# The second layer's last twelve ticks: three steps of norms, gates and experts in a tick instead of two

## The chip, the cores and the metric

The kernel runs on one core of one Trainium2 chip. The metric is the device time of one execution in microseconds (us); lower is better. Five engines work side by side, each through its own instructions in order: PE (TensorE, matmuls; its weight loads are listed apart as PEld), DVE (VectorE), ACT (ScalarE), POOL (GpSimd) and SP (SyncE, which here only starts transfers). The order of an engine's instructions is fixed when the program is built.

## The reference

Two layers, each a graph network followed by a mixture of experts, all with a residual, over 6250 nodes of 256 values. The change is in the second layer:

```python
# L1_gnn
h = relu(x @ Wp.T + bp)
hp = h ** 2
msgs = edge_vals[:, None] * hp[src]
agg = segment_sum(msgs, dst, num_segments=N) ** 0.5
x = x + (h @ W1.T + b1 + agg @ W2.T + b2)
# L1_ffn, on the layer norm of x
all_out = experts_mlp(x)             # 4 experts, 256 -> 128 -> 64 -> 256, relu between
shared = shared_mlp(x)               # 256 -> 256 -> 128 -> 256
gates = softmax(x @ gW + gb)
topv, topi = top_k(gates, 2)
x = x + shared + sum(softmax(topv) * all_out[topi])
```

There are 106250 edges, sorted by destination.

## The kernel before

The 6250 nodes lie in 49 node tiles of 128; the edges, 128 to a tile, make 831 edge tiles. The second layer works on blocks of node tiles (L2155): ten blocks of four, then three of two (40-41, 42-43, 44-45) and three of one (46, 47, 48). The edges come in groups of six tiles, 139 groups. One loop, a tick for each group, carries everything:

- `fetch` issues on POOL an indirect DMA for each edge tile (L1104): the rows `hp[src]` land in `hg`. It runs four groups ahead.
- `weights_of` builds on DVE for each edge tile a matrix `eq` of 128 edges by 96 nodes, the edge's weight where its destination is (L2390). It runs one group ahead.
- `add_up` multiplies on PE `hg` by `eq` into the PSUM tile `pe` of the block that the nodes belong to (L2411); an edge tile whose 96 nodes reach over a block's end needs two matmuls. A block is zeroed by a matmul at its start (L2406). When its last edge tile is in, it is complete.
- `roots` takes on ACT the square root of a complete block (L2428, `gt`).
- `end_of2`, one generator for each node tile, has four steps: the matmuls with W1 and W2 (`w1t`, `w2t` into a `pt`), the add into `x_all` (L2229), mean and variance (L2231, L2233), `ln_rs` (L2235) and a square root on ACT (L2236); reciprocal, `off` and the normalized tile `xn` (L2238, L2240, L2242); its transposes on PE and the copy into `b_all` on ACT (L1085, L1086); the logits on PE and DVE (L1091, L2248).
- `gates2`, one for each block, has five steps of small DVE operations, with an exponential on ACT after the first (L2259) and the fourth (L2295), up to `gate` (L2302).
- `experts2`, one for each block: eleven steps up to the last hidden layer (the shared layers `h1`, `h2` and for each expert `first` and `then`, each a matmul into a `ph` and a relu: L2318, L2326, L2331, L2340), then, once the gates are there, three steps for each node tile that multiply into `py` and add into `x_all` on DVE (L2364, L2366), and last the store to the output (L2373).

`mm` (L1091) issues all matmuls but the add-up's, so most of them have that one line. The `ph` and `py` tiles have two buffers each, `pt` has one.

Generators wait in lists: `ends` (all of them advance by one in a `step_ends`, which also starts one node tile's `end_of2` if one is due), `routes` (gates) and `layers` (experts); `advance(queue, n)` takes n steps of the first in a list. After the loop come the flag checks (L2482 to L2500). From `LATE` = 104 on, a tick has two `step_ends`, two steps of gates and four of experts; before that one, one and three. The builder then places each engine's instructions in its own order, in which neighbouring steps are interleaved. After tick 138 no group is left and the loop runs on until all lists are empty.

Square root and exponential need different function tables on ACT; a change between them shows in the profile as an `ACT_TABLE_LOAD`.

Of the kernel before, what the change touches and what calls it, by code (L numbers as in the profile page):

```python
# [841 lines left out]
def kernel(ctx: ExitStack, tc: tile.TileContext, a: dict, out: bass.AP):  # L842
# [74 lines left out]
    with ExitStack() as fast:  # L917
# [48 lines left out]
        if T1 > C1:  # L966
            V.memset(flat.bitcast(I32)[:, C1:T1], 2**24)
            n = E1 - C1 * P
# [311 lines left out]
        with ExitStack() as layer:  # L1280
# [81 lines left out]
            with (  # L1362
# [61 lines left out]
                def add_up(q):  # L1424

                    w, g = groups1[q]
                    if g == 0:
                        sums[w] = pse.tile([P, WS], F32, name="pe")
                    h, eq = hbuf[q % 2], equals.pop(q)

                    for j in reversed(range(NT)):
                        for i, k in ((1, g + NG), (0, g)):
                            lo, hi = quarters(w, k)
                            if hi - lo == 4:
                                TE.matmul(
                                    sums[w], eq[k][:, j, :], h[:, i * NT + j, :],
                                    start=g == 0 and j == NT - 1 and i == 1,
                                    stop=g == NG - 1 and j == 0 and i == 0,
                                )
                                continue  # L1440
                            for b in range(lo, hi):
                                at = slice((b - lo) * Q, (b - lo + 1) * Q)
                                TE.matmul(  # L1443
                                    sums[w][b * Q : (b + 1) * Q, :], eq[k][:, j, at],
                                    h[:, i * NT + j, :], start=g == 0 and j == NT - 1,
                                    stop=g == last_of[b] and j == 0,
                                )
# [202 lines left out]
        def advance(queue, n):  # L1650
            for _ in range(n):
                if queue and next(queue[0], queue) is queue:
                    queue.pop(0)

        layers = [experts1()]
        part = sums.tile([P, 3, T, H], BF16, name="part")
        with (
# [33 lines left out]
            def fetch(g):  # L1691
                got[g] = wk.tile([P, G, GW], F32, name="sg", bufs=5)
                for j in range(G):
                    gather(got[g][:, j, :], gat_dram, src2[:, g * G + j : g * G + j + 1])
# [447 lines left out]
            k = NA + 5  # L2142
# [14 lines left out]
        with (  # L2157
# [62 lines left out]
            def end_of2(b, i, root):  # L2220


                w = blocks[b][0] + i
                pm = psm.tile([P, D], F32, name="pt")
                mm(
                    pm, lambda c: (b_all[:, w, 0:P], root[:, i, :])[c],
                    lambda c: (w1t, w2t)[c],
                )
                V.tensor_add(x_all[:, w, :], x_all[:, w, :], pm)  # L2229
                st = wk.tile([P, 6], F32, name="ln_st")  # L2230
                V.bn_stats(st, x_all[:, w, :])  # L2231
                mv = wk.tile([P, 2], F32, name="ln_mv")
                V.bn_aggr(mv, st)  # L2233
                rs = wk.tile([P, 1], F32, name="ln_rs")
                V.tensor_scalar(rs, mv[:, 1:2], EPS, None, op0=OP.add)  # L2235
                SC.activation(rs, rs, AF.Sqrt)  # L2236
                yield
                V.reciprocal(rs, rs)  # L2238
                off = wk.tile([P, 1], F32, name="off")
                V.tensor_scalar(off, mv[:, 0:1], rs, -1.0, op0=OP.mult, op1=OP.mult)  # L2240
                xn = wk.tile([P, D], F32, name="xn")
                SC.activation(xn, x_all[:, w, :], AF.Identity, bias=off, scale=rs)  # L2242
                yield
                transposed(psm, b_all[:, w, :], xn)
                yield
                pg = psm.tile([P, D], F32, name="pt")
                mm(pg[:, 0:NX], lambda c: b_all[:, w, c * P : (c + 1) * P], lambda c: gw[:, c, :])
                V.tensor_add(logits(b)[:, i * NX : (i + 1) * NX], pg[:, 0:NX], gb)  # L2248
# [126 lines left out]
            groups2 = [range(t, min(t + G1, T1)) for t in range(0, T1, G1)]  # L2375
# [10 lines left out]
            def weights_of(k):  # L2386

                equals[k] = wk.tile([P, G1, NW], F32, name="eq", bufs=3)
                for j, t in enumerate(groups2[k]):
                    V.tensor_scalar(  # L2390
                        equals[k][:, j, :], lanes[:, 0:NW], dst_of[:, t : t + 1],
                        ew[:, t : t + 1], op0=OP.is_equal, op1=OP.mult,
                    )
# [25 lines left out]
            def roots(b):  # L2419
                n = blocks[b][1]  # L2420
                at = slice(blocks[b][0], blocks[b][0] + n)
                V.tensor_add(
                    x_all[:, at, :], x_all[:, at, :],
                    b12[:, None, :].to_broadcast([P, n, D]),
                )
                root = wk.tile([P, BT, P], F32, name="gt")[:, 0:n, :]
                pe = sums.pop(b)[:, 0 : n * P].rearrange("p (w k) -> p w k", k=P)
                SC.activation(root, pe, AF.Sqrt)  # L2428
                return [(b, i, root) for i in range(n)]

            complete, ends, coming, routes, layers, routed = [], [], [], [], [], set()
            ended = [0] * len(blocks)

            def step_ends(k):
                for item in list(ends):
                    if next(item[1], ends) is ends:
                        ends.remove(item)
                        b = item[0]
                        ended[b] += 1
                        if ended[b] == blocks[b][1]:  # L2440
                            routes.append(gates2(b))
                            layers.append(experts2(b))
                if coming and (k % 2 or coming[0][0] * BT >= small):
                    b, i, root = coming.pop(0)
                    ends.append((b, end_of2(b, i, root)))

            LATE = len(groups2) * 3 // 4

            AHEAD = 4
            for k in range(AHEAD):
# [2 lines left out]
            k = 0  # L2455
            while k < len(groups2) or complete or coming or ends or routes or layers:
                if k + AHEAD < len(groups2):
                    fetch(k + AHEAD)
                if k + 1 < len(groups2):
                    weights_of(k + 1)  # L2460
                if k < len(groups2):
                    add_up(k)
                advance(layers, 1)
                step_ends(k)
                if k >= LATE:
                    advance(layers, 1)
                    advance(routes, 1)
                while complete:
                    coming += roots(complete.pop(0))
                advance(routes, 1)  # L2470
                advance(layers, 2)
                if k >= LATE:
                    step_ends(k)
                k += 1


        with (
# [6 lines left out]
            n = wk.tile([P, NB + 7], F32, name="n")  # L2484
# [4 lines left out]
            for i in range(2):  # L2489
                k = NB + 1 + 2 * i  # L2490
# [55 lines left out]
```

## Time and profile before

| | us |
|---|---|
| runs | 3552.38, 3555.01, 3555.68 (median 3555.01) |
| profiled execution | 3555.79 |
| its span, first to last instruction | 3554.0 |
| second layer's loop: start of the first gather to the start of the last | 2467.6 to 3505.4 |
| start of the last add into `x_all` | 3544.4 |

Busy times over the whole span:

| engine | busy us | share |
|---|---|---|
| PE | 3338.9 | 94% |
| DVE | 2170.1 | 61% |
| ACT | 1412.1 | 40% |
| POOL | 2252.3 | 63% |

The shares are means over stages with different limits. In the second layer POOL issues one gather after the other, 831 of them; PE works on add-ups, norms, gates and experts in between. The mean granted clock of TensorE over the span is 0.911; in the loop from 2508 us to the end it is 0.73. Times in the text are counted from the start of the span.

### The profile page before, as it was taken

What the parts mean: (1) busy time and instruction counts of PE and PEld (TensorE: products, weight loads), DVE (VectorE), ACT (ScalarE), POOL (GpSimd) and SP (SyncE); (2) the same over time, 40 slices, a digit from 0 to 9 for tenths busy, and PEclk for the clock granted to TensorE, in tenths of its full rate; (3) what the DMA queues carried; (4) which work ended last, traced back from release to release, by engine and by line L of the source; (5) the groups of instructions that cost most, each with busy time, mean ns of one, the idle gap of its engine ahead of it and who ended that gap; (6) DMA issues with size and microseconds to landing.
All of it is one profiled execution on the core that took longest, in us unless ns stands there. A gap on an engine that the chain in (4) does not pass through costs nothing.

```text
span 3554.0 us, 57573 instructions
## 1 busy us (share of the span) xinstructions
PE 3338.9 (94%) x20063; PEld 2662.0 (75%) x20063; DVE 2170.1 (61%) x6210; ACT 1412.1 (40%) x2750; POOL 2252.3 (63%) x2367
## 2 busy tenths in 40 slices
PE   7999999999999999999999999997678988989898
PEld 3577777777777778888888888895456666666677
DVE  9999996444544444787758576977234444444464
ACT  4444444444444444444544454664011212211133
POOL 0376666666666664676656555662777777777773
PEclk9999999999999999999999999998567776777797
DMA  6456656656555554433434343553112222222221
GB/s 174 128 189 189 184 183 184 186 186 182 183 183 188 181 183 142 110 97 96 125 88 127 83 130 84 154 94 109 52 53 59 60 59 59 59 59 60 65 62 37
DMA packets 342928, 428.52 MB, mean 121 GB/s; under 512 B 139174, under 2 KB 246453, under 8 KB 342630
## 3 DMA queue, kind: packets, MB, share of 16 engines
q1 hardware_dynamic: 245174, 244.98, 22.1%
q0 software_dynamic: 89408, 178.08, 19.4%
q8 instruction: 162, 2.65, 0.3%
q10 hardware_dynamic: 8048, 1.68, 0.2%
q14 instruction: 136, 1.11, 0.1%
HBM read 382.05 MB, written 42.49 MB: 119 GB/s over the span
## 4 chain that ended last, share of the span: by engine, by line
PE 66%; POOL 14%; DMA 7%; issue 7%; DVE 4%; ACT 1%; SPq 0%; ACTq 0%; POOLq 0%; DVEq 0%
PE ph L1091 32%; POOL hg L1104 13%; PE py L1091 10%; PE pt L1085 7%; PE pe L1443 6%; PE po L1771 5%; DMA hg<-hp_dram,src 5%; PE pt L1091 2%; DMA rb<-low_dram 1%; PE pe L2411 1%; PE pa L1708 1%; PE pm L1091 1%; DVE junk L982 1%; DVE key L1240 0%; DVE order L1237 0%
## 5 line engine op out<-in xcount | busy, mean ns | idle before, releaser
L1104 POOL DMA_INDIRECT yg<-y_dram,src x882 | 847.0, 960 | 543.1 <-issue 226.7
L1104 POOL DMA_INDIRECT hg<-hp_dram,src x831 | 785.7, 946 | 269.2 <-issue 224.3
L1104 POOL DMA_INDIRECT sg<-gat_dram,src x640 | 614.1, 960 | 350.1 <-issue 161.5
L1091 PE MATMUL ph<-w1b,et 128*128 128x256 f32 x3528 | 835.7, 380 | 0.0
L1091 PEld LDWEIGHTS ph<-w1b,et 128*128 128x128 f32 x3528 | 637.0, 190 | 68.7
L2411 PE MATMUL pe<-eq,hg 128*128 128x96 f32 (+15 forms) x2036 | 439.9, 353 | 148.9 <-DMA hg<-hp_dram,src 120.6
L2411 PEld LDWEIGHTS pe<-eq,hg 128*128 128x128 f32 x2036 | 388.2, 260 | 251.8 <-issue 94.6
L1417 DVE TENSOR_TENSOR yg<-ph,yg 128x512 f32<-128x512 f32 x441 | 303.3, 688 | 375.3 <-PE ph L1091 370.7
L2390 DVE TENSOR_SCALAR eq<-px,dst,ew 128x96 f32<-128x96 f32 x831 | 262.0, 370 | 217.2 <-PE pe L2411 120.6
L1091 PE MATMUL ph<-b_all,w 128*128 128x256 f32 (+1 forms) x1600 | 387.1, 380 | 1.5 <-ACT hh L1607 1.4
L1091 PE MATMUL py<-w,hh 128*128 128x256 f32 x1568 | 383.1, 384 | 5.0 <-ACT hh L1607 4.5
L1086 ACT ACTIVATE et<-pt 128x512 f32<-128x512 f32 x441 | 262.2, 596 | 254.4 <-PE pt L1085 242.1
L1422 ACT ACTIVATE h<-yg 128x512 f32<-128x512 f32 x441 | 276.1, 626 | 215.4 <-DVE yg L1417 209.0
L1091 PEld LDWEIGHTS py<-w,hh 128*128 128x128 f32 x1568 | 288.7, 190 | 41.2 <-ACT hh L1607 6.6
L1091 PEld LDWEIGHTS ph<-b_all,w 128*128 128x128 f32 x1600 | 290.0, 190 | 33.7 <-ACT hh L1607 2.0
L1607 ACT ACTIVATE hh<-ph,b 128x256 f32<-128x256 f32 (+1 forms) x400 | 166.7, 467 | 285.6 <-PE ph L1091 279.7
L1085 PE MATMUL pt<-ident,ea 128*128 128x128 f32 x1764 | 272.1, 277 | 3.4 <-ACT et L1086 3.4
L1085 PEld LDWEIGHTS pt<-ident,ea 128*128 128x128 f32 x1764 | 210.2, 144 | 65.0 <-issue 40.4
L1771 PE MATMUL po<-pp,B 128*128 128x240 f32 (+10 forms) x1280 | 252.1, 337 | 2.2 <-DVE acc L1777 2.1
L1771 PEld LDWEIGHTS po<-pp,B 128*128 128x128 f32 x1280 | 215.6, 190 | 14.3 <-DVE acc L1777 2.8
L1443 PE MATMUL pe<-h,eq 128*32 128x257 f32 x3168 | 216.8, 384 | 3.7 <-ACT h L1422 1.9
L1443 PEld LDWEIGHTS pe<-h,eq 128*32 128x32 f32 x3168 | 96.2, 109 | 102.6 <-issue 35.0
(330 smaller groups left out, 4264.5 us busy)
## 6 DMA issues: line engine op xcount, KB each, us to landing
ea<-in_edge_attr_dram SPq DMA_DIRECT2D x147, 768.0 KB
y<-y SPq DMA_DIRECT2D x196, 128.0 KB
w<-in_L_ffn_W_dram SPq DMA_DIRECT2D x48, 512.0 KB
y<-ys SPq DMA_DIRECT2D x96, 256.0 KB
rb<-low_dram SPq DMA_DIRECT2D x80, 256.0 KB
yg<-y_dram,src POOLq DMA_INDIRECT x882
hg<-hp_dram,src POOLq DMA_INDIRECT x831
sg<-gat_dram,src POOLq DMA_INDIRECT x640
```

The lines of the kernel that those rows point to most:

```text
L982: V.tensor_scalar(junk, flat, float(w * P), None, op0=OP.is_lt, op1=OP.add, accum_out=below[:, w : w + 1],)
L1085: TE.transpose(pt[:, c, :], src[:, c * P : (c + 1) * P], ident)
L1086: SC.activation(dst, pt.rearrange("p c k -> p (c k)"), AF.Copy)
L1091: TE.matmul(dst, lhs(c), rhs(c), start=c == 0, stop=c == n - 1)
L1104: GP.indirect_dma_start(out=dst, out_offset=None, in_=table[0:NP, :], in_offset=IndirectOffsetOnAxis(ap=idx, axis=0),)
L1417: V.tensor_add(y, ph, y)
L1422: SC.activation(h[:, j : j + 2, 0:D], y, AF.Relu)
L1443: TE.matmul(sums[w][b * Q : (b + 1) * Q, :], eq[k][:, j, at], h[:, i * NT + j, :], start=g == 0 and j == NT - 1, stop=g == last_of[b] and ...
L1607: SC.activation(hidden[u][:, f, :n, :], ph[:, f - f0, :n, :], AF.Gelu, bias=b1[:, e, f : f + 1],)
L1771: TE.matmul(po.rearrange("p b v -> p (b v)"), B[:, j, :], pp[:, j, 0:n, :].rearrange("p b v -> p (b v)"), start=half == 0 and j == 0, stop ...
L2390: V.tensor_scalar(equals[k][:, j, :], lanes[:, 0:NW], dst_of[:, t : t + 1], ew[:, t : t + 1], op0=OP.is_equal, op1=OP.mult,)
L2411: TE.matmul(sums[b][:, lo - t0 * P : hi - t0 * P], hg[:, j, :], eq[:, j, lo - n0 : hi - n0], start=False, stop=after >= (t0 + n) * P,)
```

## The change

The body of the tick is written as a loop of one, two (from tick 104) or three (from tick 127, `LAST12`) rounds; a round has one step of the first experts, one `step_ends`, one step of the first gates and one more step of the experts (two in a tick before 104). The roots are taken in the first round. So from tick 127 on, also in the ticks behind the last group, a tick has three `step_ends`, three steps of gates and six of experts, where it had two, two and four. From 104 to 126 the numbers are as before, but the second step of gates comes after the second `step_ends` instead of ahead of it, and the fourth step of the experts too; in all ticks the first step of gates now comes ahead of the roots.

```diff
-            LATE = len(groups2) * 3 // 4
+            LATE, LAST12 = len(groups2) * 3 // 4, len(groups2) - 12
...
-                advance(layers, 1)
-                step_ends(k)
-                if k >= LATE:
+                for n in range(1 + (k >= LATE) + (k >= LAST12)):
                     advance(layers, 1)
+                    step_ends(k)
                     advance(routes, 1)
-                while complete:
-                    coming += roots(complete.pop(0))
-                advance(routes, 1)
-                advance(layers, 2)
-                if k >= LATE:
-                    step_ends(k)
+                    if n == 0:
+                        while complete:
+                            coming += roots(complete.pop(0))
+                    advance(layers, 2 if k < LATE else 1)
                 k += 1
```

No operation is added or removed; the same work is issued in another order.

## The prediction

> **What bounds the kernel now.** I read the chain of waits over the last 250 us first, then POOL's, PE's and DVE's timelines, then busy time and clock window by window. From 3331.9 to 3463.0 the chain is POOL issuing the gathers of L1104, one every 1.25 us, and their landing; from 3465.5 on it is PE.
>
> ```profile
> 3460.45 0.94 POOL hg L1104
> 3461.70 0.94 POOL hg L1104
> 3462.95 2.46 DMA hg<-hp_dram,src
> 3465.54 1.02 PE pe L2411 x4
> ```
>
> Columns: start, length, what. Before 3465 an earlier expert step would be ready sooner and change nothing, since PE waits for gathers anyway.
>
> ```profile
> 3505.38 0.94 POOL L1104 DMA_INDIRECT hg<-hp_dram,src  x1 [0.30 <-issue]
> 3512.81 0.36 PE L2411 MATMUL pe<-eq,hg 128*128 128x96 f32 x2
> ...
> 3544.39 0.48 DVE L2366 SCALAR_TENSOR_TENSOR x_all<-py,gate,x_all 128x256 f32<-128x256 f32 x1
> ```
>
> The last gather starts at 3505.4 and, with the 2.46 us above, lands at 3507.9. The last add-up matmul (pe) ends at 3513.2, so PE is 5 us behind the gathers. The last add into x_all ends at 3544.9; store and flag check take the other 9.1 us of the span of 3554.0, and no line of the change touches them. At stake are the 31.7 us from the last add-up to the last add, and PE's delay before.
>
> ```profile
> 3460.94:3464.35 3.41, 2.03 (x15) 1.73 (x13) 2.88 (x9) 0.00 (x0) 2.50 (x4) 1.00 0.17 49
> 3464.35:3467.76 3.41, 3.11 (x13) 2.85 (x13) 0.00 (x0) 0.00 (x0) 2.67 (x3) 0.50 0.20 58
> 3491.65:3495.06 3.41, 3.41 (x10) 2.69 (x9) 0.76 (x5) 2.30 (x4) 2.80 (x3) 0.50 0.19 58
> 3495.06:3498.47 3.41, 3.41 (x23) 3.18 (x22) 1.92 (x7) 0.88 (x2) 2.50 (x4) 0.99 0.18 52
> 3464.35:3495.06 30.71, 30.39 (x110) 27.14 (x111) 9.55 (x39) 4.80 (x11) 23.39 (x25) 0.50 0.22 62
> ```
>
> Columns: window, length, busy of PE, weight load, DVE, ACT, POOL, then granted clock, DMA share, GB/s. The clock is 1.0 or 0.5 and changes only at steps of 3.41 us. A window with PE busy 2.03 us was followed by half clock; full clock came back after a window filled with 256-column expert matmuls. Cutting everything from 2600 us on into such windows, each full-clock window with 2.2 us or less busy was followed by half clock, and none with more than 3.0. So 30.7 us before the end ran at half clock.
>
> **The change, part by part.** I number blocks by node tiles: 44-45, 46, 47, 48 are the last four.
>
> *Ticks before 127* only change order inside a tick. Cost 0: POOL's chain hides it (POOL waits for nothing but its own issue, 0.30 us each). Without that cover, one expert step of 0.4 to 0.9 us would show.
>
> *Ticks 127 to 130.* Block 42-43 is finished in tick 130 instead of 132. Ticks 131 to 133 then hold little but gathers; PE idles there and is at half clock when it leaves tick 133. The last gather of that tick is 27 before the end: 3505.4 - 27 x 1.25 + 2.5 = 3474.1, so PE, with one pe more, is free at about 3474.5. Before, the same point came at 3476.7.
>
> *From there to the last add-up.* In the built order of PE, blocks 44-45 and 46 stand ahead of the last add-up almost whole; before, five output matmuls of 44-45 and all of 46 stood behind. At full-clock durations (spacings of PE's timeline): 42 pe at 0.23 = 9.7; 28 matmuls of 256 columns at 0.43 = 12.0; four L2329 of two tiles at 0.57 = 2.3; block 46's 14 of 128 columns at 0.22 = 3.1, four at 0.36 = 1.4, four outputs at 0.43 = 1.7; transposes, logits, zeroing 2.4. Sum 32.6. Half clock lasts until a filled window. From about 3479 eight 256-column matmuls stand together, 7.1 us at the half-clock 0.89 (3490.1 to 3493.7 shows four in 3.56), long enough to hold one, so release at 3482 to 3486, I take 3484: 9.5 us at half speed, penalty 4.8. Waits for ACT 0.6 (half a table load of 1.28). New is a wait on DVE: the last tick's three eq (L2390) now stand behind node 47's add, statistics and rs (0.42 + 0.43 + 0.17 + 0.14), which wait for PE's w2t matmul of node 47; the last three pe wait for these eq: 1.2 + 0.3 for the first, 1.5 in all. Last add-up: 3474.5 + 32.6 + 4.8 + 0.6 + 1.5 = 3514.0, 0.8 later than before.
>
> *Behind it.* Before, 25.5 us of PE work, 5.3 of waits, 0.9 from the last matmul to the last add. Off go five outputs of 44-45 (2.1) and block 46 (0.9 + 1.8 + 0.45 + 1.4 + 2.2 = 6.8): 16.6 left. Waits: node 47's xn, behind the three eq (0.94), share (0.48), reciprocal and off (0.37) on DVE and 0.59 on ACT, leaves PE idle 1.6; its copy 0.45; two table loads (1.28 each) ahead of block 47's relus cost 0.9, since the third ph must wait for a relu to free one of two buffers; another ahead of block 48's relus 0.9; handoffs 0.5: 4.4. At the end the share's exp (L2295) of block 48 now stands behind ACT's last relu, before it stood ahead: exp 0.16, five DVE steps 1.0, then the four adds 2.2: 3.5 after the last matmul instead of 0.9. So 16.6 + 4.4 + 3.5 = 24.5 instead of 31.7: -7.2, with the 0.8 above -6.4.
>
> *The clock in the tail.* From w2t of node 47 to its xn are 4.0 us, in which PE has 0.9 us of work. Wherever the 3.41 us windows fall, one holds less than 2.2 us busy, and by the rows above half clock follows. Transposes, logits, h1 and the first two experts of 47 (3.7 us at full clock) then run at half until a filled window two or three later: +2.9 after what the table loads hide. Bounds: 0, and 3.7 plus as much again if the third window isn't filled. I take 2.9: **-3.5**.
>
> [...]
>
> Stores (L2373) of 42 to 47 move ahead with their blocks on SP's queue, which has nothing else there; the last store stays last. No DMA on POOL moves. If stores weren't hidden, only the last one (inside the 9.1 us) would tell.
>
> The profiled execution took 3555.8, 1.8 beyond its span; the median is 3555.0. 3555.8 - 3.5 = 3552.3 in its terms, 3551.5 for the median.
>
> **The rivals.**
> 1. *The clock holds and PE catches up with the gathers.* For it: PE stays at full clock in the row 3525.78 with 2.43 us busy, so the limit isn't sharp; ticks 131 to 133 may hold the clock through, removing the 4.8. Against it: the drought there and the 4.0 us above. Last add-up between 3508.2 (last landing plus one pe) and 3514.0, no tail penalty: -6.4 to -12.2, middle -9: 3546.
>
> ```profile
> 3525.78:3529.19 3.41, 2.43 (x18) 1.97 (x16) 2.20 (x11) 3.16 (x9) 0.00 (x0) 1.00 0.14 43
> ```
>
> 2. *Nothing gained.* PE's work is only put in another order, and PE is full from 3465: what leaves the tail (8.9) comes back as delay of the last add-up, at its bound 8.9 - 2.2 (begun earlier) = 6.7, so -0.5: 3554.5. Against it: the 30.7 us at half clock leave room.
> 3. *Slower: half clock from tick 131 to the end.* If add-ups between the expert steps keep every window from being filled (as from 3464 to 3491, busy all the time and yet half), 11 us more at half speed until 3495 cost 5.5, and a tail of 16.6 all at half about 10: -6.4 + 5.5 + 10 = +9: 3564. It decides once over 13 us of PE work more than I count run at half clock. Against it: eight large matmuls together.
>
> **How the numbers follow.** Forecast 0.41, rival one 0.40, rival two 0.09, rival three 0.10. Forecast's own range 3548 to 3554. The measurement can tell 0.2%, 7.1 us: under 3547.9 is faster, over 3562.1 slower. Rival one gives faster but for its uppermost tenth (0.36 and 0.04), forecast and rival two no change (with that 0.04, 0.54), rival three slower (0.10). The range 3543.5 to 3558 leaves out rival three and an eighth of rival one, 0.15.
>
> **What would show it.** Right: the last gather starts at 3505 as before; last add-up at 3513 to 3515; behind it PE idles some 1.5 us twice, waiting for eq and xn; a half-clock window follows; last add 24 to 29 us after the last add-up. Clock 1.0 throughout the tail is rival one, a last add-up at 3519 or later rival two or three. Wrong altogether if the gathers' spacing grows: then the ticks before 127 weren't free.

## The result, and the profile after

| | before | after |
|---|---|---|
| median of 20 runs, us | 3555.12 (3550.81 to 3560.97) | 3560.34 (3555.28 to 3566.59) |
| ratio of the medians, 95% interval | | 1.0015 (1.0008 to 1.0022) |
| profiled execution, us | 3555.79 | 3566.08 |
| its span | 3554.0 | 3564.3 |
| start of the first gather of the loop | 2467.64 | 2472.49 |
| start of the last gather | 3505.38 | 3512.49 |
| end of the last add-up matmul | 3513.2 | 3527.3 |
| end of the last add into `x_all` | 3544.9 | 3555.4 |

The changed kernel is slower by 2.8 to 7.8 us. The prediction was 3551.5, a gain, with a range up to 3558.0; the measured median is 2.3 us above that. The profiled execution of the changed kernel is within 0.5 us of its slowest run. It enters the loop 4.9 us later, though nothing ahead of the loop was changed, and its gathers take 2.3 us longer. Of that, 2.1 us had come together by gather 780, before a tick with three rounds had begun, and e18 below, which has the same order up to there, took 1037.5 us from the first to the last gather where the kernel before took 1037.7; so this part is scatter between executions. So I compare distances from the start of the last gather, and take 7.1 us (3512.49 - 3505.38) off the times of after to set them beside those of before. From the last gather's start to the end of the span it is 48.6 before and 51.8 after: 3.2 us of the loss lie in the part that the change touches, by this one pair of profiles.

Two windows of each kernel hold nearly all of that. The first reaches from the zeroing of block 44-45's sums (a matmul of L2406, 3375.3 before and 3381.7 after) to the last add-up matmul, the second from there to the last add. Columns as in the prediction: window, length, busy of PE with its matmul records, weight load, DVE, ACT, POOL, then granted clock. Before:

```profile
3375.30:3513.20 137.90, 134.36 (x655) 106.78 (x655) 74.60 (x296) 49.01 (x94) 99.07 (x105) 0.85 0.21 59
3513.20:3544.90 31.70, 29.02 (x168) 22.01 (x167) 21.07 (x105) 20.44 (x51) 0.00 (x0) 1.00 0.05 17
```

After:

```profile
3381.70:3527.30 145.60, 140.64 (x707) 110.39 (x706) 81.04 (x325) 56.10 (x110) 99.72 (x106) 0.88 0.22 58
3527.30:3555.40 28.10, 23.06 (x114) 17.31 (x114) 15.69 (x77) 14.17 (x35) 0.00 (x0) 0.84 0.03 10
```

Some 53 matmul records went from the second window to the first (168 to 114, 655 to 707). What to look at is PE's busy time beside the length: before, PE was busy 134.4 of the first 137.9 us. There was no hole for the work that came.

Cutting both windows where the granted clock changes tells how much of the busy time ran at half clock. In the kernel before four matmuls of 256 columns take 3.56 us at half clock (3490.09 to 3493.65) and two take 0.87 at full (3497.00 to 3497.87), so I call busy time less half of that the *work*, in us at full clock; length = work + idle + half-clock time / 2.

| us | length | work | idle | at half clock |
|---|---|---|---|---|
| before, to the last add-up | 137.9 | 114.1 | 3.5 | 40.5 |
| after, to the last add-up | 145.6 | 123.9 | 5.0 | 33.5 |
| before, behind it | 31.7 | 29.0 | 2.7 | 0 |
| after, behind it | 28.1 | 19.3 | 5.0 | 7.6 |

The work is conserved: 114.1 + 29.0 = 143.1 before, 143.2 after. To the last add-up: 9.8 more work, 1.4 more idle, 3.5 less for half clock (7.0 / 2), 7.7 longer. Behind it: 9.8 less work, 2.4 more idle, 3.8 more for half clock, 3.6 shorter. The first window starts 0.7 earlier against the last gather, and the end behind the last add is 0.2 shorter: 7.7 - 3.6 - 0.7 - 0.2 = 3.2.

Where the clock went in after, by the same windows of 3.41 us:

```profile
3474.70:3478.11 3.41, 3.41 (x14) 2.96 (x12) 2.82 (x11) 0.53 (x2) 2.53 (x3) 0.50 0.42 125
...
3488.35:3491.76 3.41, 3.41 (x10) 2.69 (x9) 0.02 (x1) 0.82 (x2) 2.49 (x4) 0.51 0.20 50
3491.76:3495.18 3.42, 3.42 (x21) 2.86 (x20) 1.51 (x9) 2.33 (x6) 2.51 (x4) 1.00 0.18 46
...
3505.42:3508.83 3.41, 2.80 (x25) 2.66 (x24) 3.35 (x13) 0.75 (x2) 2.49 (x4) 0.99 0.21 55
3508.83:3512.24 3.41, 3.41 (x17) 3.41 (x18) 0.22 (x2) 0.37 (x1) 2.74 (x3) 0.50 0.22 58
3512.24:3515.66 3.42, 3.42 (x13) 2.97 (x13) 1.15 (x3) 0.80 (x3) 0.94 (x1) 0.52 0.24 38
3515.66:3519.07 3.41, 3.41 (x24) 2.94 (x22) 3.09 (x10) 0.95 (x3) 0.00 (x0) 1.00 0.00 0
...
3525.89:3529.31 3.42, 2.48 (x14) 1.89 (x14) 3.14 (x15) 1.21 (x4) 0.00 (x0) 0.99 0.00 0
3529.31:3532.72 3.41, 3.13 (x13) 3.06 (x14) 0.99 (x4) 0.76 (x3) 0.00 (x0) 0.50 0.11 38
```

Three stretches at half clock: the one that began with the drought of ticks 131 to 133 (the ticks that hold little but gathers), a new one from 3508.7 to 3515.6, and the tail's. (One more, at the start of the first window, stands in both kernels, to 3385.9 before and to 3392.7 after, and from 3553.1 on, behind the last wait, the last two matmul records run at half clock.) PE's timeline shows what stands at their beginnings (last column: idle time before the group, and what ended it):

```profile
3506.17 0.65 PE L2411 MATMUL pe<-eq,hg 128*128 128x46 f32 x4 [0.61 <-DVE eq L2390]
...
3526.27 1.03 PE L2411 MATMUL pe<-eq,hg 128*128 128x96 f32 x6 [1.67 <-DVE eq L2390]
3527.66 0.39 PE L2479 MATMUL pg<-good,ones 128*128 128x8 f32 x2 [0.37 <-ACT gt L2428]
...
3529.59 1.01 PE L1091 MATMUL pt<-gw,b_all 128*128 128x4 f32 x4 [0.47 <-ACT b_all L1086]
...
3553.68 1.19 PE L1091 MATMUL py<-ew,g 65*128 65x256 f32 x2 [2.26 <-DVE miss L2488]
```

PE waits for `eq` twice, 0.61 and 1.67 us: DVE builds it in its own order, the second time behind the add and the norm steps of node tile 47 that the third round put ahead of it, the first time behind an add (L2364) and the gate steps. The kernel before has a wait like the first, also behind an add, in a window from 3505.31 on with 2.83 us busy, and kept the full clock:

```profile
3506.91 0.68 PE L2411 MATMUL pe<-eq,hg 128*128 128x1 f32 x4 [0.58 <-DVE eq L2390]
```

So the wait alone does not explain the stretch at 3508.7. The 2.26 at the end is the share of the last block: a `py` buffer comes free only when an add with the gate is done (the releaser named, a flag check's step, stands beside those adds in DVE's order).

### The profile page after: what moved, and what is told of

It reads as the page before. It is cut to its first block, busy times and chain, and to the rows that moved or that the text cites. A ratio compares the mean times of both kernels' runs of the same rounds, so it can differ in the third digit from the quotient of the medians.

```text
span 3564.3 us, 57555 instructions
## 1 busy us (share of the span) xinstructions
PE 3334.0 (94%) x20063; PEld 2653.1 (74%) x20063; DVE 2171.8 (61%) x6210; ACT 1412.8 (40%) x2750; POOL 2257.6 (63%) x2367
## 4 chain that ended last, share of the span: by engine, by line
PE 68%; POOL 12%; issue 7%; DMA 6%; DVE 5%; ACT 2%; SPq 1%; ACTq 0%; DVEq 0%; POOLq 0%
PE ph L1091 32%; POOL hg L1104 12%; PE py L1091 10%; PE pt L1085 7%; PE pe L1443 6%; PE po L1771 5%; DMA hg<-hp_dram,src 3%; PE pt L1091 3%; PE pe L2411 2%; DMA rb<-low_dram 2%; PE pa L1708 1%; PE pm L1091 1%; DVE eq L2390 1%; DVE junk L982 0%; DVE x_all L1952 0%
## 5 line engine op out<-in xcount | busy, mean ns | idle before, releaser
L2411 PEld LDWEIGHTS pe<-eq,hg 128*128 128x128 f32 x2036 | 379.1, 255 | 265.3 <-issue 101.9
```

Source lines behind the costliest of these rows:

```text
L2411: TE.matmul(sums[b][:, lo - t0 * P : hi - t0 * P], hg[:, j, :], eq[:, j, lo - n0 : hi - n0], start=False, stop=after >= (t0 + n) * P,)
```

## The experiments

Theory A: the clock is what the prediction missed; without the new half-clock stretches the change would gain. Theory B: PE is full ahead of the last add-up, so whatever moves there delays it one for one, and the tail, a chain of waits, gives back less. Theory C: it is `eq`, built too late. The expectations use other names: their theory A joins A and B (the third round puts work ahead of the last add-ups, and PE's waits there cost the clock), R1 is the new order inside the ticks, R2 the third round behind the last group, and R3 is theory C. Their distances from the last gather (7 to 9 or 14 to 15.5 us) were meant for a chip like that of the result.

One thing has to be known of the first sixteen runs. They ran on chips on which the kernel before itself takes 4317 to 4361 us. In their profiles PE, DVE and ACT stop at times for several us without a releaser in the trace (PE 8.5 us at once in e12, DVE 8.4 and ACT 14.0 in e13); the chain of waits of the changed kernel there reads

```profile
PE 60%; another core or an unknown queue 13%; DVE 11%; issue 8%; ACT 4%; POOL 2%; DMA 1%; ACTq 0%; SPq 0%; DVEq 0%; POOLq 0%
```

The loop's gathers take 1221 to 1244 us instead of 1038, and PE ends its add-ups 28 to 58 us behind the last gather instead of 8 to 15. Ratios are good to some 0.3% there, twice the effect. What can be read there is what doesn't hang on the pauses: matmul counts, PE's work, and the tail with its clock. The last two runs came on a chip that takes 3555 to 3557.

| run | edit | ratio to before (95%) | last add-up to last add, us |
|---|---|---|---|
| e1 | two rounds | 1.0004 (0.9978 to 1.0030) | 29.95 |
| e3 | third only behind the last group | 1.0017 (0.9996 to 1.0038) | 29.94 |
| e6 | the same | 1.0016 (0.9989 to 1.0043) | 29.95 |
| e2 | third only in ticks 127 to 138 | 1.0045 (1.0024 to 1.0066) | 28.88 |
| e5 | the same | 1.0035 (1.0008 to 1.0062) | 28.11 |
| e13 | the changed kernel | 1.0020 (0.9991 to 1.0049) | 28.10 |
| e4 | `eq` a group earlier | 1.0041 (1.0014 to 1.0068) | 30.95 |
| e7 | the same | 1.0076 (1.0052 to 1.0100) | 30.95 |
| e8 | zero matmuls in the last wait | 1.0048 (1.0022 to 1.0075) | 25.10 |
| e9 | zero matmuls in ticks 132, 133 | 0.9994 (0.9960 to 1.0028) | 28.64 |
| e10 | both, and one in tick 136 | 1.0016 (0.9991 to 1.0041) | 25.44 |
| e14 | the same | 1.0024 (1.0000 to 1.0048) | 25.45 |
| e12 | norms and gates only | 0.9994 (0.9970 to 1.0018) | 24.15 |
| e15 | the same | 1.0015 (0.9990 to 1.0040) | 23.10 |
| e11 | before, zero matmuls in tick 132 | 1.0002 (0.9971 to 1.0033) | 31.71 |
| e16 | the same | 0.9998 (0.9979 to 1.0017) | 31.70 |
| e17 | before (chip at 3557.25) | one run, 3554.96 | 31.70 |
| e18 | gates first (same chip) | one run, 3552.81 | 25.96 |

### The change in halves (e1, e2, e3, e5, e6, e13)

```diff
-                for n in range(1 + (k >= LATE) + (k >= LAST12)):
+                for n in range(1 + (k >= LATE)):                                     # e1
+                for n in range(1 + (k >= LATE) + (LAST12 <= k < len(groups2))):      # e2, e5
+                for n in range(1 + (k >= LATE) + (k >= len(groups2))):               # e3, e6
```

e1: 

> The tick is written as in the changed kernel, but there is never a third round: only the order inside a tick differs from before. Theory A (the third round in ticks 127 to 138 puts expert work ahead of the last add-ups, and PE's waits there cost the clock): as before, ratio 0.999 to 1.0005, last add-up 7 to 9 us after the last gather's start (before 7.8, changed kernel 14.8). Rival R1 (the new order inside the ticks costs it): ratio 1.001 or more, last add-up late as in the changed kernel.

e2: 

> Third round in ticks 127 to 138 alone, two rounds behind the last group. Theory A: as the changed kernel or a little better, ratio 1.001 to 1.002, last add-up 14 to 15.5 us after the last gather's start. Rival R2 (the third round behind the last group costs it, by gates that come late and table loads): ratio 1.000.

e3: 

> Third round behind the last group alone. Theory A: ratio 0.9985 to 1.0005, last add-up 7 to 9 us after the last gather's start, 29 to 32 us from there to the last add. Rival R2: ratio 1.001 or more.

e5: 

> Third round in ticks 127 to 138 alone, again, since the chip of the first four runs stopped all engines at times for reasons the profile doesn't show and took 4361 us for the kernel before. On a chip that takes about 3555 us, theory A (the third round in ticks 127 to 138 puts expert work ahead of the last add-ups and PE's waits there cost the clock): ratio 1.001 to 1.002, last add-up 14 to 15.5 us after the last gather's start (before 7.8). Rival R2 (the third round behind the last group costs it): ratio 1.000.

e6: 

> Third round behind the last group alone, again. Theory A: ratio 0.9985 to 1.0005, last add-up 7 to 9 us after the last gather's start, 29 to 32 us from there to the last add. Rival R2: ratio 1.001 or more. Rival R1 (the new order inside the ticks costs it, which this kernel has too): last add-up 12 us or more after the last gather's start.

e13: 

> The changed kernel once more, on the same chip as the three beside it. If its loss is of the order of work: 1.0010 to 1.0025 of the kernel before. If it is chance in where the clock's windows fall: 0.999 to 1.001.

e3 and e6 are built into the same order of instructions as e1 on all five engines: a third round once the groups are over changes nothing, since there its lists are drained in the same order anyway. So 1.0004, 1.0017 and 1.0016 are one kernel measured three times, and show what a ratio is worth there. The third round in ticks 127 to 138 carries what effect there is: both runs of it lie above 1 with their intervals, and e2 and e5 have the changed kernel's order of instructions, so that they and e13 are one kernel measured three times too (1.0045, 1.0035 and 1.0020). First the windows of e1, then those of e5; the ends of the windows are chosen as above.

```profile
4163.70:4329.80 166.10, 145.37 (x666) 113.34 (x666) 75.73 (x302) 50.88 (x97) 75.94 (x81) 0.80 0.15 39
4329.80:4359.80 30.00, 26.88 (x157) 20.09 (x155) 19.23 (x99) 18.51 (x49) 0.00 (x0) 1.00 0.05 18
```

```profile
4120.90:4297.30 176.40, 152.12 (x707) 116.63 (x706) 81.24 (x325) 56.21 (x110) 76.13 (x81) 0.80 0.14 38
4297.30:4325.40 28.10, 23.04 (x115) 17.17 (x114) 15.67 (x77) 14.20 (x35) 0.00 (x0) 0.83 0.03 10
```

41 records more ahead of the last add-up make that window 10.3 us longer, and taking them from the tail makes it 1.9 shorter. That is theory B's picture, though with pauses in it: the first windows' idle times, 20.7 and 24.3, differ by more than one could call an effect. e13 by itself (1.0020, its interval reaches below 1) can't tell order from chance. Clearer is the stretch from the last gather's start to the last add-up, in which PE idles little (1.6 to 5.6 us): PE's work there is 28.2, 28.2 and 29.7 us in e1, e3 and e6, and 34.6, 35.9 and 35.5 in e5, e13 and e2; the last add-up ends 38.5 to 40.6 us behind that start in the first three, 48.0, 48.0 and 57.5 in the others (e2 has 38 us at half clock there, the others 15 to 19).

### Building `eq` a group earlier (e4, e7)

```diff
-                equals[k] = wk.tile([P, G1, NW], F32, name="eq", bufs=3)
+                equals[k] = wk.tile([P, G1, NW], F32, name="eq", bufs=4)
...
             weights_of(0)
+            weights_of(1)
...
-                if k + 1 < len(groups2):
-                    weights_of(k + 1)
+                if k + 2 < len(groups2):
+                    weights_of(k + 2)
```

e4: 

> The changed kernel with the add-up weights (eq) built two groups ahead and in four buffers, so that on DVE the last group's three no longer stand behind node 47's statistics. Rival R3 (this wait of PE for eq, 1.7 us, and the one of 0.6 us in tick 136 ahead of a half-clock stretch, are the cost): last add-up 9 to 11 us after the last gather's start, ratio 0.999 to 1.000. Theory A in the form that expert work ahead in PE's order costs it whatever the eq do: 13 to 14.5 us, ratio 1.001 or more.

e7: 

> The changed kernel with the add-up weights (eq) built two groups ahead and in four buffers, again. Rival R3 (PE's waits for eq are the cost): last add-up 9 to 11 us after the last gather's start, ratio 0.999 to 1.000. Theory A in the form that expert work ahead in PE's order costs it whatever the eq do: 13 to 14.5 us, ratio 1.001 or more.

Slower than before in both, with intervals wholly above 1. The edit did not take the wait away: ahead of the last add-up PE still waits for `eq`, 3.7 us at once in e4 and 4.4 in e7. And the tail, with the same work as in the changed kernel (19.5), has 8.3 us of idle instead of 5.1, as this answer on PE's waits in e7's tail shows (waiting for whom, total us, times, longest):

```profile
PE py L1091 <- DVE x_all L2366: 2.4, 1, 2.4
PE py L1091 <- DVE miss L2489: 2.3, 1, 2.3
PE ph L1091 <- ACT h L2340: 1.1, 1, 1.1
```

The first of these is not there in e5. From the last gather's start to the last add are 80.8 and 81.4 us, where e5 and e13 have 76.1 (e2, with its 38 us at half clock, 86.4). So this way out of the wait costs more than it saves; theory C itself is not tested by it, since the wait stayed.

### Zero matmuls to hold the clock (e8, e9, e10, e14, and e11, e16 in the kernel before)

They multiply `ident` by zeros: into an unused `pe` buffer behind the last block's root (e8), or into the open sums ahead of add-up matmuls, where they add nothing (the others). Nothing is left out.

```diff
 def roots(b):
+                if b == len(blocks) - 1:                      # e8, e10, e14
+                    warm = pse.tile([P, BT * P], F32, name="pe")
+                    for _ in range(6):
+                        TE.matmul(warm[:, 0:D], ident, nothing[:, 0:D], start=True, stop=True)
...
 def add_up(k):
+                        if k in (132, 133):                   # e9; e10, e14: or k == 136 and j == 0; e11, e16: k == 132
+                            TE.matmul(sums[b][:, 0 : n * P], ident, nothing[:, 0 : n * P],
+                                      start=False, stop=False)
```

e8: 

> The changed kernel with six more matmuls of 256 columns on zeros into a free buffer of the add-up's PSUM pool, results unused; the built order puts five of them into PE's wait for the last three eq and one behind the first of the last add-ups. If the clock in the tail is lost because PE waits there (theory A): clock 1.0 through that wait and behind it, last add 24 to 26 us after the last add-up instead of 28.1, and the time 2 to 3 us under the changed kernel's, ratio 1.0005 to 1.001. If the half clock there costs nothing: 2 us more, ratio 1.0015 to 1.002.

e9: 

> The changed kernel with a 128-column matmul of ident by zeros (adds nothing to the sums) ahead of each add-up matmul of ticks 132 and 133, 19 in all, 4.2 us at full clock, where PE waits for gathers. If the first half-clock stretch (3474.7 to 3491.8 in the profile of after) is what makes the last add-up late, it goes: 8.5 us of half speed saved less at most 3 us of filler that the waits don't hide, so the last add-up ends 6 to 10 us (not 14.8) behind the start of the last gather, and the time is 4 to 6 us under the changed kernel's. If the work of the third round by itself makes it late, the clock holds there but the last add-up stays 13 us or more behind the last gather, and the time stays within 2 us of the changed kernel's. If filler only costs: 2 to 4 us over.

e10: 

> As before, with one more zero matmul ahead of the first add-up matmul of tick 136 (where PE waited 0.61 us for eq ahead of the second half-clock stretch) and six of 256 columns in PE's wait for the last eq. If the clock is what the prediction missed: no half clock from tick 132 to the last add, last add-up 4 to 8 us behind the start of the last gather, last add 24 to 26 us behind that, the time 8 to 12 us under the changed kernel's and 3 to 6 us under the kernel before. If it is the order of the work: only the tail's 3 us are gained, and the time is not under the kernel before.

e14: 

> The changed kernel with 20 zero matmuls of one node tile's 128 columns in ticks 132, 133 and 136 and six of 256 columns in PE's wait for the last eq. If the clock is what the prediction missed: no half clock from tick 134 to the last add, and 6 to 12 us under the changed kernel beside it. If it is the order of the work: 2 to 4 us under it, for the tail alone.

e11: 

> The kernel before with the same zero matmuls ahead of the 10 add-up matmuls of tick 132 (2.2 us at full clock), where its half-clock stretch of 30.7 us began. If the clock alone decides when the last add-up ends: no half clock ahead of 3495, last add-up 3 to 4 us behind the start of the last gather instead of 7.8, and the time 3 to 5 us under the kernel before. If PE, having caught up, waits for gathers and falls to half clock a few windows later: last add-up at 7 us or more, the time within 2 us of the kernel before.

e16: 

> The kernel before with zero matmuls ahead of the 10 add-up matmuls of tick 132. If its half-clock stretch sets the end: 3 to 5 us under the kernel before. If PE then waits for gathers and loses the clock later: within 2 us.

In the tail the clock's price is shown. The second window of e8, beside that of e5 above, has the same count of matmul records:

```profile
4296.70:4321.80 25.10, 19.63 (x115) 14.29 (x114) 15.26 (x73) 13.86 (x35) 0.00 (x0) 1.00 0.03 11
```

1.00 instead of 0.83, and 25.1 us instead of 28.1; in e10 and e14 25.4. So half clock in the tail costs 2.7 to 3.0 us; the prediction had 2.9. The fillers have a price ahead of it: from the start of node tile 47's matmuls with W2 to the end of the last add-up are 3.8 us in e8, 3.3 in the changed kernel of the result. Ahead of the last add-up the fillers did not do what theory A wanted: in e9, e10 and e14 half clock still held for 14 to 20 us that end 33 us ahead of the last gather's start, and for 20 us around that start (52.6 to 60.6 us at half clock in the first window, 52.8 in the changed kernel there). Where fillers stood they did not keep PE busy: in e9 the later of these stretches begins at 4246.61, inside the filled ticks, behind a window in which PE waits without a releaser in the trace:

```profile
4243.20:4246.61 3.41, 1.64 (x9) 1.35 (x8) 0.00 (x0) 0.00 (x0) 2.80 (x3) 1.00 0.22 58
```

The ratios tell nothing from before or from one another. e11 and e16, one program, show how much chance the clock holds there: from the zeroing of block 46's sums to the last add-up 32.3 us at half clock in one and 9.4 in the other, 100.5 against 86.4 us long. Whether theory A holds for the stretch at 3508.7 on a chip like the first was not tried.

### Norms and gates without the expert steps (e12, e15)

```diff
-                    advance(layers, 1)
+                    advance(layers, int(n < 2))
...
-                    advance(layers, 2 if k < LATE else 1)
+                    advance(layers, 2 if k < LATE else int(n < 2))
```

e12: 

> The changed kernel's third step of norms and gates from tick 127 on without its two expert steps: the experts run no earlier than with two rounds. If the expert work moved ahead of the last add-ups is what makes them late: last add-up 7 to 9 us behind the start of the last gather as in the kernel before, last add 30 to 32 us behind that, time within 2 us of the kernel before. If norms and gates (DVE's and ACT's steps ahead of eq) make them late: last add-up 11 us or more behind the last gather and the time 3 us or more over the kernel before.

e15: 

> Third step of norms and gates from tick 127, no third pair of expert steps. If the expert work that moved ahead of the last add-ups makes them late: within 2 us of the kernel before, and 4 us or more under the changed kernel beside it. If norms and gates do: like the changed kernel.

Neither branch of the expectation came. The expert steps don't stay where they were: with the norms ready sooner, two rounds of experts bring as much ahead of the last add-up as three did. Windows of e15:

```profile
4140.10:4325.00 184.90, 156.46 (x721) 121.17 (x721) 80.59 (x329) 56.18 (x113) 76.08 (x81) 0.79 0.13 37
4325.00:4348.10 23.10, 18.20 (x102) 13.47 (x101) 14.48 (x72) 13.29 (x33) 0.00 (x0) 0.95 0.04 12
```

721 and 102 records, where the changed kernel has 707 and 115 (e13): the tail is 5 us shorter, the window ahead of it 3 us longer, the ratio cannot be told from 1. The norms' early end is enough by itself to let the work come forward; expert steps without norms were not tried.

### The kernel before again, and the gates first (e17, e18)

```diff
-                    advance(routes, 1)
+                    advance(routes, 1 + (k >= len(groups2)))         # e18
```

e17: 

> The kernel before, profiled where gathers come 1.47 us apart. If the changed kernel only moves PE's work ahead of the last add-up, PE's work between the zeroing of block 42-43's sums and the last add-up, half-clock time counted half, is 114 us as in the first profile of this kernel (124 to 125 in the changed one), and behind the last add-up 29 us (19.3 in the changed one). If the changed kernel makes or saves work, the two sums differ by over 1 us.

e18: 

> The changed kernel with two gate steps a round behind the last group, so that block 48's gate shares stand ahead of its last relus. If the share behind the last relu makes the end late, as the prediction has it (3.5 us from the last matmul group to the last add where 0.9 stood before): last add 25 to 26 us behind the last add-up instead of 28.1. If PE would have to wait for the share's place elsewhere, or for the four adds: 27.5 us or more.

These two came on one chip with the times of the first result. The stretch begins at the zeroing of block 44-45's sums, as in the result above (e17's expectation calls it 42-43). Windows of e17:

```profile
3375.10:3512.50 137.40, 133.02 (x655) 105.14 (x655) 74.58 (x296) 49.04 (x94) 99.45 (x106) 0.86 0.22 59
3512.50:3544.20 31.70, 29.08 (x169) 22.07 (x167) 21.07 (x105) 20.43 (x51) 0.00 (x0) 1.00 0.05 17
```

Windows of e18:

```profile
3371.30:3516.30 145.00, 137.44 (x707) 107.60 (x706) 81.10 (x325) 56.06 (x110) 99.23 (x106) 0.91 0.22 58
3516.30:3542.20 25.90, 22.77 (x114) 17.30 (x114) 15.39 (x76) 13.93 (x35) 0.00 (x0) 0.86 0.03 11
```

| us | length | work | idle | at half clock |
|---|---|---|---|---|
| e17, to the last add-up | 137.4 | 114.7 | 4.4 | 36.6 |
| e18, to the last add-up | 145.0 | 124.9 | 7.6 | 25.1 |
| e17, behind it | 31.7 | 29.1 | 2.6 | 0 |
| e18, behind it | 25.9 | 19.6 | 3.1 | 6.4 |

Both pairs of profiles agree, and the sums of the work, 143.8 and 144.5, differ by less than the 1 us that e17's expectation set. The work moved is 9.8 and 10.2, the first window grows by 7.7 and 7.6; the last add-up ends 7.8 and 6.9 us behind the last gather's start in the kernel before, 14.8 and 14.7 with the third round. In e18 half clock held from 4.3 us ahead of that start to 2.5 behind it, in after from 3.8 to 3.1: the stretch that the prediction lacked came again at its place, in another pair of profiles. And e18's tail is 2.1 us shorter than after's, with the share's exponential ahead of the last relu:

```profile
3539.21 0.70 PE L1091 MATMUL py<-ew,g 65*128 65x256 f32 x2
3540.68 0.67 PE L1091 MATMUL py<-ew,g 65*128 65x256 f32 x2 [0.77 <-DVE miss L2488]
```

0.77 us of wait where after had 2.26. e18's single time, 3552.81, is under its neighbours' 3554.96 and 3557.25, but it entered the loop at 2464.1 where e17 did at 2468.7; from the last gather's start to the end it took 49.4, e17 47.6. It isn't shown to beat the kernel before. Gates first and the filled last wait together would by these parts give some 49.4 - 3.0 + 0.5 = 46.9 (an estimate from e18 and e8, with 0.5 for the fillers ahead of the last add-up); that was not run.

## Why the prediction was wrong

**The step that failed** is "From there to the last add-up", its sum of 3514.0, "0.8 later than before". Measured on the scale of before it is 3520.2 (3527.3 - 7.1), 7.0 later. Its terms, measured from 3482.2, where PE is done with tick 133's add-ups, to 3527.3 in after, and beside them those of the kernel before (3476.7 to 3513.2):

| term | before | predicted | measured |
|---|---|---|---|
| PE free behind tick 133 | 3476.7 | 3474.5 | 3475.1 |
| PE's work up to the last add-up | 26.7 | 32.6 | 34.3 |
| waits | 0.6 | 2.1 | 3.1 |
| half speed | 9.2 | 4.8 | 7.7 |
| last add-up | 3513.2 | 3514.0 | 3520.2 |

All four terms err the same way: 0.6 + 1.7 + 1.0 + 2.9 = 6.2. The sum let 5.9 us of added work be paid for mostly by 4.4 less for half clock; 7.6 came in, and half clock gave back 1.5. The term most off is half speed, by a second half-clock stretch, 6.8 us long, 3.4 of delay, that the sum had at nothing; the first, with its release at 3484, came as said (3491.7 - 7.1 = 3484.6). I had looked for thin windows in the drought and in the tail, not ahead of the last add-up. Why the clock was lost there isn't shown: PE's wait for `eq` of 0.61 us stands in the window ahead of it, but the kernel before bore one of 0.58. The `eq` wait that I did foresee was 1.67 for 1.5.

**The balance that was not made** would have warned. I counted what leaves the tail, and separately what stands ahead of the last add-up, but not that PE was busy 134.4 of 137.9 us there. By length = work + idle + half-clock time / 2, work brought into a full stretch comes out as delay unless idle time or half clock shrinks there, and both are on view: 3.5 us idle and 40.5 at half clock before. Rival two said just that, with "at its bound 8.9 - 2.2 = 6.7" for the delay: measured 7.0. It then took the tail's -7.2 without the clock loss that my own forecast had, or it would have come to 6.7 - 7.2 + 2.9 = +2.4, close to the +3.2 of the profiles. The nearness of 6.7 to 7.0 is partly luck: measured are 9.8 more work, 1.4 more idle, 3.5 less for half clock, from a start 0.7 earlier, and rival two had 8.9 and 2.2 alone. By the prediction's own sign, a last add-up at 3519 or later, it was rival two or three. I gave rival two 0.09. Two things that I knew, a full PE ahead and a half clock behind, stood in different cases and never in one sum.

**What was right.** The tail: predicted 24.5 + 2.9 = 27.4, measured 24.3 (work and idle) + 3.8 = 28.1. The reason given for its half clock, a window with less than 2.2 us busy, was not quite met: in after the window 3522.38:3525.80 had 2.22 and kept the full clock, and half clock followed the next, with 2.48; in e18 it followed one with 2.18. The half-clock windows in it, priced at 2.9, cost 2.7 to 3.0 by e8, e10 and e14; the share behind the last relu, priced at 3.5 - 0.9 = 2.6, cost 2.1 by e18. Gathers keep their spacing (1.2503 and 1.2530 us; 1.2492 and 1.2499 in e17 and e18), so the ticks before 127 were free in that respect. Of the two waits foreseen, that for `xn` is not there: PE waits 0.37 us for `gt`, and the flag check's matmuls (L2479) and a `py` stand ahead of the last transpose.

**Rival one** (the clock holds and PE catches up) failed at the second stretch and in the tail. **Rival three** (half clock from tick 131 to the end) failed: the release at 3491.7 came.

Neither half-clock stretch that the third round brought follows a long wait: in the 7 us ahead of the new one and of the tail's, PE's longest waits were 0.61 and 1.67 us.

What stays open: why the clock is lost at 3508.7, how much of the loss that stretch makes by itself (3.4 us by its length; no run took it alone away on a chip like the first), and 2 us of the measured 5.2 that these profiles, at 3.2, don't show but the interval (2.8 to 7.8) allows.

## What to carry to other kernels

Before moving work ahead of a point, ask how idle the engine is there: with PE busy 97% of the stretch, 9.8 us moved forward made it 7.7 longer, though half clock took 3.5 less of it, and the tail that lost them, a chain of handoffs, shrank by 3.6. Add up work, idle and half clock on both sides of the point in one balance, and price every thin window on the way, not only those at the ends. And compare distances from a common event: four profiles of kernels that are the same up to the loop entered it 8 us apart (2464.1 to 2472.5), more than the effect.

## What the runs showed of the hardware

PE's busy share of a window does not settle whether half clock follows. In after, a window with 2.80 us busy was followed by it; in the kernel before, this one was not:

```profile
3505.31:3508.72 3.41, 2.83 (x16) 1.82 (x14) 2.51 (x10) 3.38 (x8) 0.94 (x1) 1.00 0.26 43
```

Nor was one with 2.43 (shown in the prediction). In that profile, from 2600 us on, windows with 2.2 or less always were, but not in after, where the first window here, with 1.53, was followed by full clock:

```profile
3262.97:3266.38 3.41, 1.53 (x5) 0.90 (x6) 3.10 (x15) 0.00 (x0) 2.50 (x4) 1.00 0.17 41
3266.38:3269.80 3.42, 3.42 (x9) 1.52 (x8) 2.76 (x12) 1.38 (x2) 2.57 (x3) 1.00 0.22 58
```

What decides is not known from these runs. From 2600 us on each return to full clock came behind a window with PE busy 3.3 us or more (26 returns before, 29 after), but not each such window was followed by one: before, 3467.76:3471.18 and the next two were busy throughout and half clock went on to 3495.1. With five zero matmuls of 256 columns in one wait the granted clock was 1.00 through a tail of 25.1 us (e8), without them 0.83 in one of 28.1 (e5). And the same program, the kernel before, took 3555 us on some chips and 4317 to 4361 on others, where the traces have stops that they put to no instruction of this kernel: 8.5 us (PE, e12), 8.4 (DVE, e13) and 14.0 (ACT, e13).
